# Reordering the query blocks and spreading the projections of an attention and memory kernel

## The chip, the cores and the metric

The kernel runs on one core of a Trainium2 chip. The metric is the device time of one launch in microseconds (us). Engines are called as the profile calls them: PE (matrix multiplication; PEld is its weight load), DVE (vector), ACT (scalar, with the exponentials), POOL (general), SP (here: the queue that issues nearly all DMAs). All data are 32-bit floats.

## The reference

Four sequences (B = 4) of S = 1024 tokens with C = 256 channels pass through four residual steps:

```python
x = x + attn_a(layernorm(x), ...)   # 16 heads of 16 channels, own LayerNorm inside, out-projection with bias
x = x + ffn(layernorm(x), W)        # W rounded to -1, 0, 1 times its mean absolute value
x = x + attn_b(layernorm(x), ...)   # a memory of two 64x64 matrices, updated token by token
x = x + ffn(layernorm(x), W)
```

`attn_a` is full softmax attention: `scores = q k^T / 4`, softmax over the 1024 keys, times v, times `w_out` plus `b_out`, plus its own input. `attn_b` works through the tokens in chunks of 128: keys, values and queries are projections with a causal convolution over four tokens, the gradient of a squared loss of the two matrices at each token is clipped in norm, and two linear recurrences over the tokens (with per-token rates alpha, eta, theta that are themselves means of sigmoids and a softplus of projections) give the matrices that each token's query is answered with. Chunk c needs the state left by chunk c-1 of all four sequences.

## The kernel before, in words

**The main loop.** Queries come in four blocks of 256 (k = 0 to 3), heads in two pairs of groups. A *unit* is (block k, batch b, pair of head groups): 4 x 4 x 2 = 32 units, listed in `units` (L184) with k outermost and b inside it. A unit goes through eight key chunks `kc`, each in two *halves* (`half`, L1207). A half issues, in this order on PE:
- `maxima` (L234): two matmuls of 512 columns (`mx`, L244) for a unit that comes ten key chunks later; DVE reduces them to negated row maxima (`nm`, L248). After a unit's last maxima `maxima_rows` (L250) turns them (`ng`, `nt`), writes them to DRAM (`d`) and reads them back as one row of the queries' tile (`qslot`), so the later scores come out with their maximum subtracted;
- `scores` (L270): eight matmuls of 256 columns (`sc`, L278), whose exponentials ACT takes (`pt`, L284);
- side work (below), after the first half only;
- `weigh` (L288): exponentials times values (`av`, L298), one key chunk late.

The PE, DVE and ACT streams run in the order in which the program issues them; the order of the SP and POOL streams is left to the scheduler of the framework.

**Side work.** Everything else is written as generators that yield between pieces and wait in named *lanes* (`lanes`, L438). `beside(PACE)` (L459) runs pieces of the lanes, in lane order, until a budget of columns is spent: `PACE` = 1200 columns are added per key chunk, and each PSUM tile that a piece takes with `mps` is charged the number given there. If it spent fewer than `LIGHT` = 500, `weigh` is split over the two halves; otherwise it comes whole after the second. `through(lane, ...)` (L477) does the opposite of pacing: it runs all pieces of a lane up to a key at once, between two scores.

**What the side work is.** `project(b)` (L1084) makes a batch's queries, keys and values: load x (two tiles of 4 x 128 tokens), LayerNorm statistics on DVE (L1096, L1097), eight small POOL operations on them (L1102 to L1108, `rr`), the normalised tile `h` on DVE (L1116), 16 transposes on PE (`hps`, L1124), 16 matmuls of 512 columns for queries and keys (`cps`, L1133; ACT adds the bias, SP writes them to DRAM), 16 of 256 for values (`vps`, L1151), and last six long POOL operations that leave x + bias + attention residual in `X` (L1169 to L1172). `other_weights` (L1035) makes the output bias `bo` and the rounded ffn weight; `memory_setup` (L884) loads and transposes the weights of `attn_b` (`wps`, `wpst`, L889; `wops`, `gwps`). `finish` (out-projection `po`, ffn `pf`, both L395), `theta`, `prepare`, `advance`, `retrieve` and `output` do the rest of the layers for a query block once its units are through.

**Where the projections sit.** Batch 0's come before the loop. Those of batches 1, 2 and 3 wait in the lane `before`, and in each unit of the first block this line is met at the fourth key chunk (L1233):

```python
if u + 2 < n0:                                    # n0 = 8, the units of block 0
    through("before", lambda key: key <= units[u + 2][1])
```

So unit 0 runs what is left of batch 1, unit 2 that of batch 2 together with `memory_setup`, and unit 4 that of batch 3, each in one burst between two halves. PE's PSUM is shared as two tiles for maxima (`x`), one for `av` and three for everything else (`m`: scores and side work).

Of the kernel before, what the change touches and what calls it, by code (L numbers as in the profile page):

```python
# [16 lines left out]
P = 128  # L17
# [18 lines left out]
def tile_hybrid(ctx: ExitStack, tc: tile.TileContext, x, ln_gamma, ln_beta, w_qkv, b_qkv, w_out, b_out,  # L36
# [100 lines left out]
    xsp = ctx.enter_context(tc.tile_pool(name="xsp", bufs=1))  # L137
# [41 lines left out]
    def extra(t):  # L179
# [3 lines left out]

    units = [  # L184
        (k, b, tuple(range(g, g + N5 // w)))
        for k, (t0, w) in enumerate(BLOCKS)
        for b in range(B)
        for g in range(0, NG, N5 // w)
# [177 lines left out]
    def finish(b, t, m=2, buf=None):  # L366
# [10 lines left out]
        def turned(src, name):  # L377

            ps = mps([P, 2, m, P], f"{name}p_{n}", 256)
            for e in ts:  # L380
                for cc in range(2):
                    T.transpose(ps[:, cc, e, :], src[:, e, cc * P : (cc + 1) * P], ident)
            if name == "hdT" and t in hids:
                for e in ts:
                    A.copy(hids[t + e][:, :, b, :], ps[:, :, e, :])
                return hids[t][:, :, b : b + 1, :]
            dst = buf("tT", name)[:, :m, :].rearrange("p e c -> p (e c)").rearrange("p (c e t) -> p c e t", c=2, e=m)
            A.copy(dst, ps)  # L388
            return dst

        def times(srcT, w, name):
            ps = mps([P, m, C], f"{name}_{n}", 1024)
# [12 lines left out]

        Xi = X[:, b, t : t + m, :]
# [14 lines left out]
        through("before", lambda key: key <= 2)  # L421
# [4 lines left out]
        tps = mps([P, m, P], f"tps_{n}", 512)  # L426
# [12 lines left out]
        "settle", "finish", "theta", "memory", "ready", "answers", "last", "outputs", "before"  # L439
# [19 lines left out]
    def beside(pace):  # L459

        at["due"] = min(at["due"] + pace, 1500)
        done = 0
        for lane in lanes:
            while lanes[lane] and lanes[lane][0][1] <= at["now"] and at["due"] >= 1 and done < 700:
# [17 lines left out]
    def theta(k, cs):  # L482
# [20 lines left out]
        ps = mps([P, m, 2, 2], f"thp_{k}_{cs.start}", 256)  # L503
# [32 lines left out]
    def prepare(c, g, own):  # L536
# [34 lines left out]
        ps = mps(full, f"natp_{c}", 256)  # L571
# [18 lines left out]
        pa = mps(full, f"pa_{c}", 512)  # L590
# [4 lines left out]
        pe = mps(full, f"pe_{c}", 256)  # L595
# [61 lines left out]
    def advance(c, g, box, own):  # L657
# [86 lines left out]
        if not last:  # L744
# [20 lines left out]
            pw = mps([D, B, D], f"pw_{c}", 160)  # L765
# [42 lines left out]
    def output(c, box, groups, op, add):  # L808
# [23 lines left out]
        for p in pairs:  # L832
            ps = mps([P, 2, C], f"ops_{c}_{p.start}", 512)
# [31 lines left out]
        for p in pairs:  # L865
            ps = mps([P, 2, 2, P], f"oth_{c}_{p.start}", 256)
# [16 lines left out]

    def memory_setup(sp):  # L884

        def transposed(dst, src, rows, name):
            for cc in range(2):
                ps = mps([P, P], f"{name}{cc}")
                T.transpose(ps[:, :rows], src[:rows, cc * P : (cc + 1) * P], ident[:rows, :rows])  # L889
                V.tensor_copy(dst[:, cc, :], ps[:, :rows])  # L890

        with nc.allow_non_contiguous_dma(reason="small constants"):
# [8 lines left out]
            nc.sync.dma_start(b_t[:D, :], tb.rearrange("(p o) -> p o", o=1))  # L901
            nc.sync.dma_start(b_t[D:, :], tb.rearrange("(p o) -> p o", o=1))
# [11 lines left out]
        tn = sp.tile([D, C], F32, tag="nat", name="tn")  # L914
        nc.sync.dma_start(tn, tW)
        transposed(wt, tn, D, "wpst")
        yield 1
# [54 lines left out]
    with tc.manual_schedule(engines=OWN):  # L972
        share(m=8)
        with ExitStack() as s1_:
# [60 lines left out]
            def other_weights(sp):  # L1035

                fw = sp.tile([P, 2, C], F32, name="fw")
                bor = sp.tile([P, C], F32, name="bor")
                nc.sync.dma_start(wo, w_out.rearrange("(cc p) n -> p cc n", p=P))
                nc.sync.dma_start(fw, ffn_w.rearrange("(oc p) i -> p oc i", p=P))  # L1040
# [3 lines left out]
                bvb = sp.tile([P, 2, P], F32, name="bvb")  # L1044
# [6 lines left out]
                yield 1  # L1051
                ones = sp.tile([P, P], F32, name="ones")
# [18 lines left out]
                for ic in range(2):  # L1071
                    ps = mps([P, C], f"fps{ic}")
# [11 lines left out]
            def project(b):  # L1084

                hT = hTp.tile([P, 2, S], F32, tag="hT", name=f"hT_{b}")
# [4 lines left out]
                mv = small.tile([P, NT, 2], F32, tag="mv_a", name=f"mv_a{b}", bufs=1)  # L1091
                r = small.tile([P, 6, NT], F32, tag="rr", name=f"rr_a{b}", bufs=1)
                if b:
                    yield 2
# [14 lines left out]
                yield 3  # L1109
                hs = []  # L1110
                for hf in range(2):
                    h = lnp.tile([P, 4, C], F32, tag="h", name=f"h_{b}_{hf}")
                    hs.append(h)
                    for i in range(4):
# [4 lines left out]
                        if i % 2:  # L1119
                            yield 1 + i // 2  # L1120
                    for cc in range(2):
                        ps = mps([P, N5], f"hps_{b}_{hf}_{cc}", 256)
# [3 lines left out]
                        yield 1  # L1126
                for n in (0, 2, 1, 3):
                    dst = (dq if n < 2 else dk)[b][(n % 2) * P : (n % 2) * P + P, :]
                    for hf in range(2):
                        o = slice(hf * N5, (hf + 1) * N5)  # L1130
                        ps = mps([P, N5], f"cps_{b}_{n}_{hf}", 1024)
                        for cc in range(2):
                            T.matmul(  # L1133
                                ps, lhsT=wg[:, cc, n * P : (n + 1) * P], rhs=hT[:, cc, o], start=cc == 0, stop=cc == 1
                            )
                        c = cmp_.tile([P, N5], F32, tag="c", name=f"c_{b}_{n}_{hf}")
                        A.activation(c, ps, AF.Identity, bias=bqk[:, n : n + 1])  # L1137
                        nc.sync.dma_start(dst[:, o], c)
                        yield 1
                    if b == 0 and n > 1:  # L1140
                        yield "half"
# [4 lines left out]
                for i in range(0, NT, 2):  # L1146
                    ps = mps([P, 2, C], f"vps_{b}_{i}", 1024)
                    for e in range(2):
# [6 lines left out]
                    for e in range(2):  # L1155
# [5 lines left out]
                    yield 1  # L1161
                for g in range(2):
                    nc.sync.dma_start(dv[b][g], v[:, g])
                if b == 0:
                    yield "values"

                for hf, h in enumerate(hs):
                    Xh = X[:, b, 4 * hf : 4 * hf + 4, :]
                    G.tensor_add(Xh, xts[b, hf], bo.unsqueeze(1).to_broadcast([P, 4, C]))  # L1169
                    rh = r[:, 5, 4 * hf : 4 * hf + 4]  # L1170
                    G.tensor_mul(h, h, rh.unsqueeze(2).to_broadcast([P, 4, C]))
                    G.tensor_add(Xh, Xh, h)  # L1172
# [30 lines left out]

            LIGHT, PACE = 500, 1200
# [20 lines left out]
            n0 = sum(1 for k, _, _ in units if k == 0)  # L1225

            def unit(u):
                nonlocal late
                for kc in range(NT):
                    if kc == 0:  # L1230
                        load_keys(u + 1, range(1, 4))
                    if kc == 3:
                        if u + 2 < n0:  # L1233
                            through("before", lambda key: key <= units[u + 2][1])
# [4 lines left out]
                    for pr in range(2):  # L1239
                        half(u, kc, pr)  # L1240
                        if pr == 0:
                            light = beside(PACE) < LIGHT
# [13 lines left out]
            def memory():  # L1256
                for k, (t0, w) in enumerate(BLOCKS[:-1]):
# [4 lines left out]
                    for c in range(c0, c1):  # L1262
# [7 lines left out]
                        if c + 1 < c1:  # L1270
                            load_hid(c + 1)
                            yield 1

            def rest():
# [30 lines left out]
                def ready():  # L1305
                    for c in cs:
# [3 lines left out]
                def chain():  # L1310
                    for c in cs:
# [5 lines left out]

                for c in cs:
# [4 lines left out]
                for c in cs:  # L1323
                    if c + 1 < NT:
                        start("outputs", output(c, box, [slice(0, B)], to_put(c), G.tensor_add))
                    else:
                        of = lambda name, c: ptp.tile([P, B, C], F32, tag="pt", name=f"{name}_{c}")
                        start("last", output(c, box, [slice(0, 2), slice(2, 4)], of, V.tensor_add))

            first = project(0)  # L1330
            for _ in range(5):
                next(first)
            scaled_weights()
            for u in range(2):
                while next(first) != "half":
                    pass
# [3 lines left out]

            def values_first():
                yield from iter(lambda: next(first), "values")
                load_values(0)

# [66 lines left out]
```

## Time and profile before

| | |
|---|---|
| time, median of 3 | 1528.07 us (1520.89 to 1533.3) |
| profiled execution: time, span in the profile | 1524.56 us, 1522.7 us |
| mean granted PE clock | 0.957 |
| PE, DVE, ACT, POOL busy | 94%, 65%, 51%, 17% of the span |
| first scores of unit 0 | 73.7 us |
| units 0 to 9 | 414.8 us |
| units 10 to 29 | 816.3 us |
| unit 30 to the end | 217.9 us |

The page of the profile lists busy times, the span in 40 slices, the DMA queues, the chain of work that ended last, and the costliest groups of instructions as "line engine operation out<-in shapes xcount | busy, mean ns | idle before, what ended it". The trace behind it can be asked for a stretch of time: busy time of each engine, the granted PE clock, the waits, and the single instructions. The rows on unit times above come from the starts of the `mx` and `sc` matmuls in the trace.

### The profile page before, as it was taken

Reading aid. Unit: us, or ns where it says so; the run is one execution under the profiler, and the core shown is the slowest. Engines: PE = TensorE matmul, PEld = TensorE weight load, DVE = VectorE, ACT = ScalarE, POOL = GpSimd, SP = SyncE. Lnnn points to the kernel's source line nnn. Section 1 sums busy time; section 2 is a strip of 40 time slices with the busy share of each in tenths; the row PEclk is TensorE's granted clock in tenths of the full one; section 3 lists DMA queues with packets and bytes.
Section 4 is the critical chain, followed back from the end, with each engine's and each line's share of the span. In section 5 each row is a group of like instructions: output and inputs, shape, how many; then the busy total and the mean of one; then the engine's idle time right before and its main releaser. Section 6 shows DMA issues by size and latency. Waiting matters only on the chain.

```text
span 1522.7 us, 31195 instructions
## 1 busy us (share of the span) xinstructions
PE 1424.4 (94%) x12544; PEld 859.5 (56%) x12544; DVE 987.9 (65%) x1491; ACT 776.4 (51%) x1465; POOL 259.6 (17%) x424
## 2 busy tenths in 40 slices
PE   5979979999999999999999999999999999996886
PEld 3345545565555466565654665666554665664664
DVE  2746628467777785767576867766777767632564
ACT  2034615546565554655566556555566556563242
POOL 6340211200000110112010201210102102111232
PEclk9769979999999999999999999999999999998887
DMA  4512331332122212211213111212222112101000
GB/s 118 154 53 96 98 104 47 101 93 57 54 66 72 65 47 56 64 47 50 71 50 98 57 53 27 59 51 62 56 85 64 55 46 63 39 16 42 21 8 28
DMA packets 82100, 94.91 MB, mean 62 GB/s; under 512 B 32472, under 2 KB 62488, under 8 KB 81956
## 3 DMA queue, kind: packets, MB, share of 16 engines
q1 hardware_dynamic: 81684, 92.14, 20.7%
q8 instruction: 99, 1.62, 0.5%
q10 hardware_dynamic: 272, 0.79, 0.1%
q14 instruction: 45, 0.37, 0.1%
HBM read 60.30 MB, written 30.38 MB: 60 GB/s over the span
## 4 chain that ended last, share of the span: by engine, by line
PE 83%; DVE 7%; ACT 4%; issue 1%; POOL 1%; DMA 1%; SPq 0%; DVEq 0%; POOLq 0%; ACTq 0%
PE mx L244 20%; PE sc L278 19%; PE av L298 16%; PE cps L1133 4%; PE opf L876 2%; DVE nm L248 2%; PE pf L395 2%; PE po L395 2%; PE vps L1151 2%; ACT pt L284 2%; PE gps L820 1%; PE qqps L545 1%; PE tps L428 1%; PE vkps L545 1%; PE hps L1124 1%
## 5 line engine op out<-in xcount | busy, mean ns | idle before, releaser
L284 ACT ACTIVATE pt<-sc 128x512 f32<-128x512 f32 x1024 | 555.3, 594 | 518.0 <-PE sc L278 518.0
L248 DVE TENSOR_REDUCE nm<-mx 128x2 f32<-128x1024 f32 x512 | 619.9, 1221 | 232.4 <-PE sc L278 203.3
L278 PE MATMUL sc<-qslot,kslot 32*128 32x256 f32 x4096 | 647.7, 407 | 4.9 <-ACT m L593 2.5
L244 PE MATMUL mx<-kslot,qslot 32*128 32x512 f32 x2048 | 586.2, 656 | 6.7 <-DVE nm L248 5.7
L278 PEld LDWEIGHTS sc<-qslot,kslot 32*128 32x128 f32 x4096 | 405.5, 187 | 49.8 <-ACT pt L284 9.7
L298 PE MATMUL av<-pt,v 128*32 128x256 f32 x4096 | 302.8, 393 | 4.5 <-DVE a L306 4.4
L244 PEld LDWEIGHTS mx<-kslot,qslot 32*128 32x128 f32 x2048 | 155.9, 187 | 216.5 <-issue 131.0
L298 PEld LDWEIGHTS av<-pt,v 128*32 128x32 f32 x4096 | 96.0, 109 | 150.6 <-issue 114.3
L71 POOL TENSOR_TENSOR rso_hn<-rsi_hn,nhalf 128x2 f32<-128x2 f32 (+1 forms) x17 | 12.0, 707 | 285.0 <-DVE rsi_hn L70 237.4
L1133 PE MATMUL cps<-hT,wg 128*128 128x512 f32 x128 | 56.5, 600 | 0.0
L1160 DVE COPY vtile<-vps 128x256 f32<-128x256 f32 x24 | 9.1, 420 | 58.8 <-PE vps L1151 40.6
L71 POOL TENSOR_TENSOR rso_hd<-rsi_hd,nhalf 128x2 f32<-128x2 f32 (+1 forms) x17 | 12.0, 707 | 193.9 <-DVE rsi_hd L70 124.2
L1133 PEld LDWEIGHTS cps<-hT,wg 128*128 128x128 f32 x128 | 24.5, 194 | 29.3 <-issue 28.5
L876 PE MATMUL opf<-ffn,ohT 128*128 128x256 f32 x128 | 37.2, 440 | 3.0 <-ACT ohT L871 3.0
L1137 ACT ACTIVATE c<-cps,bqk 128x512 f32<-128x512 f32 x32 | 22.0, 687 | 34.3 <-PE cps L1133 30.2
L877 DVE TENSOR_TENSOR gt<-X,opf 128x512 f32<-128x512 f32 x16 | 11.0, 687 | 43.1 <-PE opf L876 43.1
L395 PE MATMUL pf<-ffn,hnT 128*128 128x256 f32 x124 | 32.0, 401 | 2.3 <-ACT hnT L388 2.3
L876 PEld LDWEIGHTS opf<-ffn,ohT 128*128 128x128 f32 x128 | 26.3, 216 | 12.1 <-ACT ohT L871 4.2
L395 PE MATMUL po<-wo,aT 128*128 128x256 f32 x128 | 32.3, 394 | 0.0
L820 PE MATMUL gps<-gwT,hid 128*128 128x256 f32 x128 | 31.2, 389 | 0.2 <-ACT pt L284 0.2
L1151 PE MATMUL vps<-wg,hT 128*128 128x256 f32 x128 | 29.2, 382 | 0.0
L395 PEld LDWEIGHTS pf<-ffn,hnT 128*128 128x128 f32 x124 | 22.7, 194 | 10.1 <-issue 5.0
(354 smaller groups left out, 1460.0 us busy)
## 6 DMA issues: line engine op xcount, KB each, us to landing
v<-dv SPq DMA_DIRECT2D x32, 604.0 KB
kslot<-dk SPq DMA_DIRECT2D x256, 64.0 KB
da<-a SPq DMA_DIRECT2D x31, 256.0 KB
dv<-vtile SPq DMA_DIRECT2D x8, 604.0 KB
x<-in_L_attn_a_x_dram SPq DMA_DIRECT2D x8, 512.0 KB
dq<-c SPq DMA_DIRECT2D x16, 256.0 KB
qslot<-dq SPq DMA_DIRECT2D x256, 16.0 KB
dk<-c SPq DMA_DIRECT2D x16, 256.0 KB
```

Source lines behind the costliest of these rows:

```text
L71: G.tensor_tensor(out=r[:, :n], in0=t[:, :n], in1=nhalf[:, :n], op=ALU.pow)
L244: T.matmul(ps[:, e, :], lhsT=qS[u][o : o + SL, j * P : (j + 1) * P], rhs=kt[o : o + SL, hf * N5 : (hf + 1) * N5], start=True, stop=True,)
L248: V.tensor_reduce(nms[u][:, hf, 2 * pr : 2 * pr + 2, j], ps, AX.X, ALU.max, negate=True)
L278: T.matmul(ps[e][:, g * w : (g + 1) * w], lhsT=kS[u, g][o : o + SL, kc * P : (kc + 1) * P], rhs=qS[u][o : o + SL, g * w : (g + 1) * w], st ...
L284: A.activation(pt[:, e, :], ps[e], AF.Exp, scale=1.0 / HD**0.5)
L298: T.matmul(avs[u][SL * i : SL * (i + 1), part * w : (part + 1) * w], lhsT=v[:, kc, o : o + SL], rhs=pts[u, kc, i // 2][:, i % 2, part * w ...
L395: T.matmul(ps[:, e, :], lhsT=srcT[:, cc, e, :], rhs=w[:, cc, :], start=cc == 0, stop=cc == 1)
L545: T.matmul(ps, lhsT=w[:, cc, :], rhs=hidT[:, cc], start=cc == 0, stop=cc == 1)
L820: T.matmul(ps[:, e, :], lhsT=hidT[:, cc, p.start + e, :], rhs=gwT[:, cc, :], start=cc == 0, stop=cc == 1)
L876: T.matmul(pf[:, e, :], lhsT=hT[:, cc, e, :], rhs=ffn[:, cc, :], start=cc == 0, stop=cc == 1)
L1133: T.matmul(ps, lhsT=wg[:, cc, n * P : (n + 1) * P], rhs=hT[:, cc, o], start=cc == 0, stop=cc == 1)
L1151: T.matmul(ps[:, e, :], lhsT=hT[:, cc, o : o + P], rhs=wg[:, cc, 2 * C :], start=cc == 0, stop=cc == 1,)
```

## The change

- **Order of units.** Block 1 of batch 0 is put directly behind block 0 of batch 0; the others keep their order. `n0` becomes 10 and the last unit of block 0 is unit 9.
- **Projections.** `project` is split: `input_stats(b)` (loads, statistics, the eight POOL operations) is a generator in a lane of its own, `stats`, started one batch ahead; `project` waits for it. For batches 1 to 3 the queries and keys come in pieces of 256 columns instead of 512 (32 matmuls a batch instead of 16), the values one tile of 128 tokens a piece. `through` at the fourth key chunk is replaced by `needed(b, stage)`, which runs pieces of a batch only up to the stage that the coming units need: queries and keys of the first pair of groups, of both, and values.
- **Residual sums.** The six long POOL operations move from the end of `project` to right behind each half of `h`; batch 0's stay behind the output bias.
- **Weights.** `other_weights` is split into `output_bias` (before the loop) and `last_weights`; `theta_setup` is cut out of `memory_setup`; these three go into a new lane `weights`, last in line, and are no longer run in a burst.
- **Pacing.** 900, 1000 and 1250 columns per key chunk for units 0 to 11, 12 to 23 and the rest; unspent budget up to 3000 columns instead of 1500; up to 800 columns a time instead of 700 (more while over 2000 are due); the charges of many tiles are set anew. The lane order changes.

The diff, cut to its core:

```diff
     units = [
-        (k, b, tuple(range(g, g + N5 // w)))
-        for k, (t0, w) in enumerate(BLOCKS)
-        for b in range(B)
-        for g in range(0, NG, N5 // w)
+        (k, b, tuple(range(g, g + N5 // BLOCKS[k][1])))
+        for k, b in sorted(((k, b) for k in range(len(BLOCKS)) for b in range(B)), key=lambda o: (o[0] if o != (1, 0) else 0, o[1]))
+        for g in range(0, NG, N5 // BLOCKS[k][1])
     ]
...
     lanes = {name: [] for name in (
-        "settle", "finish", "theta", "memory", "ready", "answers", "last", "outputs", "before"
+        "settle", "finish", "theta", "outputs", "memory", "ready", "answers", "last", "stats", "before", "weights"
     )}
...
-        at["due"] = min(at["due"] + pace, 1500)
+        at["due"] = min(at["due"] + pace, 3000)
...
-            while lanes[lane] and lanes[lane][0][1] <= at["now"] and at["due"] >= 1 and done < 700:
+            while lanes[lane] and lanes[lane][0][1] <= at["now"] and at["due"] >= 1 and (done < 800 or at["due"] > 2000):
...
-            def project(b):
-
-                hT = hTp.tile([P, 2, S], F32, tag="hT", name=f"hT_{b}")
+            def input_stats(b):
+
                 for hf in range(2):
                     if (b, hf) not in xts:
                         load_x(b, hf)
...
                 if b:
-                    yield 2
+                    yield 6 if b == 1 else 3
                 for i in range(NT):
                     V.bn_stats(st[:, i, :], xts[b, i // 4][:, i % 4, :])
                     V.bn_aggr(mv[:, i, :], st[:, i, :])
...
+                normed_by[b] = mv, r
+
+            def residual_sums(b, hf, h):
+
+                mv, r = normed_by[b]
+                Xh = X[:, b, 4 * hf : 4 * hf + 4, :]
+                rh = r[:, 5, 4 * hf : 4 * hf + 4]
+                G.tensor_mul(Xh, h, rh.unsqueeze(2).to_broadcast([P, 4, C]))
+                G.tensor_add(Xh, Xh, bo.unsqueeze(1).to_broadcast([P, 4, C]))
+                G.tensor_add(Xh, Xh, xts[b, hf])
+
+            def project(b):
+
+                hT = hTp.tile([P, 2, S], F32, tag="hT", name=f"hT_{b}")
+                while b not in normed_by:
+                    yield 0.5
+                mv, r = normed_by[b]
                 hs = []
...
+                    if b:
+                        residual_sums(b, hf, h)
...
+                if b and b + 1 < B:
+                    start("stats", input_stats(b + 1))
                 for n in (0, 2, 1, 3):
                     dst = (dq if n < 2 else dk)[b][(n % 2) * P : (n % 2) * P + P, :]
-                    for hf in range(2):
-                        o = slice(hf * N5, (hf + 1) * N5)
-                        ps = mps([P, N5], f"cps_{b}_{n}_{hf}", 1024)
+                    w = N5 if b == 0 else N5 // 2
+                    for o in range(0, S, w):
+                        ps = mps([P, w], f"cps_{b}_{n}_{o}", 2 * w)
...
+                    if n > 1:
+                        reached[b] = n - 1
...
-                for hf, h in enumerate(hs):
-                    Xh = X[:, b, 4 * hf : 4 * hf + 4, :]
-                    G.tensor_add(Xh, xts[b, hf], bo.unsqueeze(1).to_broadcast([P, 4, C]))
-                    rh = r[:, 5, 4 * hf : 4 * hf + 4]
-                    G.tensor_mul(h, h, rh.unsqueeze(2).to_broadcast([P, 4, C]))
-                    G.tensor_add(Xh, Xh, h)
+            def needed(b, stage):
+
+                while reached.get(b, 0) < stage:
+                    piece("stats" if lanes["stats"] and b not in normed_by else "before")
...
-            LIGHT, PACE = 500, 1200
+            LIGHT = 500
+            PACES = (900, 1000, 1250)
...
-                        if u + 2 < n0:
-                            through("before", lambda key: key <= units[u + 2][1])
+                        for v, stage in ((u + 2, 1), (u + 1, 3)):
+                            if v < U:
+                                needed(units[v][1], min(stage + units[v][2][0] // 2, 3))
...
-                            light = beside(PACE) < LIGHT
+                            light = beside(pace(u)) < LIGHT
...
-                start("before", values_first(), -1)
-                start("before", sums_first(sp2), 0)
+                start("before", first, 0)
                 for b in range(1, B):
                     start("before", project(b), b)
-                    if b == 2:
-                        start("before", memory_setup(sp2), b)
                 for _ in range(NT + LEAD):
                     for pr in range(2):
                         half(None, None, pr)
                         beside(1000)
-                through("before", lambda key: key < 0)
+                needed(0, 3)
+                load_values(0)
+                start("weights", last_weights(*setting), 0)
+                start("weights", theta_setup(*setting), 0)
+                start("weights", memory_setup(*setting), 1)
```

## Prediction

> **What bounds the kernel now.** I read the page first, then the stretches of the main loop, then who PE waits for, then the inside of the three bursts. Five lines of the page:
>
> ```profile
> PE 1424.4 (94%) x12544; PEld 859.5 (56%) x12544; DVE 987.9 (65%) x1491; ACT 776.4 (51%) x1465; POOL 259.6 (17%) x424
> ...
> PE   5979979999999999999999999999999999996886
> ...
> PEclk9769979999999999999999999999999999998887
> ...
> PE 83%; DVE 7%; ACT 4%; issue 1%; POOL 1%; DMA 1%; SPq 0%; DVEq 0%; POOLq 0%; ACTq 0%
> ```
>
> PE carries the chain and is full nearly everywhere, so time can only be won where PE is idle, where its clock is low, or where its matmuls stall. Past the start (slices 1, 2) and before the end, slices 3 and 6 (38 us each) are such places, by their PE or PEclk digit: they hold the bursts of units 0 and 2. PE's waits in the stretch 73 to 500 us (us, times, longest) name the causes:
>
> ```profile
> PE hps L1124 <- DVE h L1116: 10.3, 1, 10.3
> PE wps L889 <- DMA nat<-in_L_attn_b_eW_dram: 3.3, 1, 3.3
> PE wps L889 <- DMA nat<-in_L_attn_b_Wq_dram: 3.1, 1, 3.1
> ...
> PE wpst L889 <- DMA tn<-in_L_attn_b_tW_dram: 2.2, 1, 2.2
> ```
>
> Now the windows (stretch, length, busy us of PE, PEld, DVE, ACT, POOL, granted clock, DMA):
>
> ```profile
> 158.64:162.23 3.59, 3.59 (x45) 2.02 (x41) 3.17 (x6) 2.17 (x5) 0.00 (x0) 1.00 0.02 2
> 324.54:329.65 5.11, 5.11 (x53) 3.33 (x49) 3.55 (x8) 2.29 (x5) 0.00 (x0) 1.00 0.17 39
> 86.31:126.11 39.80, 29.51 (x127) 18.06 (x123) 12.62 (x35) 10.71 (x18) 17.38 (x13) 0.83 0.28 90
> 90.50:100.70 10.20, 0.00 (x0) 0.00 (x0) 5.09 (x20) 0.46 (x1) 4.37 (x7) 0.60 0.00 0
> 100.70:106.80 6.10, 6.03 (x20) 4.42 (x21) 2.19 (x7) 2.35 (x4) 3.61 (x2) 0.54 0.55 172
> 183.41:219.37 35.96, 27.43 (x113) 16.19 (x109) 8.84 (x28) 8.07 (x13) 6.55 (x3) 0.90 0.41 132
> 219.37:229.71 10.34, 10.34 (x61) 4.62 (x60) 5.24 (x19) 2.67 (x5) 0.00 (x0) 0.53 0.05 13
> 286.80:310.30 23.50, 23.50 (x97) 13.98 (x93) 4.69 (x10) 8.29 (x14) 4.24 (x2) 1.00 0.38 113
> ```
>
> In order: a plain pair of halves; a pair that also holds one `po`; burst 1 with its pair; its idle gap and the cold clock behind it; burst 2; the cold clock behind it; burst 3. The last has PE full at clock 1.00: a burst as such loses nothing, its waits do.
>
> **The change part by part** (against the profiled 1524.56 us; span 1522.7).
>
> *Burst 1, unit 0.* Its pair would take 3.59, `hps` 2.3 (16 transposes, 0.58 for four in the paced halves), `cps` and `vps` 20.8 (the trace: 13.74 and 7.0 in burst 2). 39.8 - 26.7 = **13.1 lost**: 10.3 idle while DVE does eight bn_stats/bn_aggr pairs (90.88 to 95.2), POOL the eight `rr` operations (95.56 to 100.3, two powers of 1.67 each) and DVE the first `h` (100.21); the other 2.8 is the clock. In the changed program the statistics come from the lane `stats`, two tiles between two maxima, a unit before the `hps`: the chain of 10 us lies beside about ten halves of PE. Uncovered it would cost the 10.3 again.
>
> *Burst 2, unit 2.* The projections end at 206.4; from there to 219.37 `memory_setup` takes 13.0 for about 2.5 of transposes at full clock. The three halves after it take 4.72, 3.03, 2.59 where 1.65, 1.94, 1.88 is usual: 4.9. Together **15.4 lost**. In the changed order each pair of `wps` stands one key chunk (over 3.6 us) behind the one that frees its `nat` tile; the waits were 3.1 and 3.3 long. I take all of it as gained; if SP is late with these loads, up to 5 comes back.
>
> [...] The window 90.50 to 100.70 has no matmul, and the clock stays near one half to 106.8: 6 us. Behind burst 2 it is 0.53 over 10.34 us. [...] The rows give 2.8 + 4.9 = 7.7. [...]
>
> *Burst 3* has nothing to win in waits.
>
> *Pacing instead of bursts.* A plain pair is 3.59 though its matmuls need less: the second half stands about 0.29 until `pt` frees a scores tile. A pair with a `po` (4 matmuls of 256 columns) takes 5.08 to 5.11: 1.5 more, while the same columns in a burst took 13.74/8 = 1.72. So a key chunk that takes projection work wins about 0.23. The changed order of PE has such pieces in about 31 key chunks of units 1 to 7: **-7**. The splitting of `cps` into 256 columns is in the price of `po`, which has that shape. Five of eight `vps` pieces still run together at the fourth key chunk of units 3, 5 and 7, at burst price.
>
> *Start.* Batch 1's `x` loads now stand in SP's queue, with four `qslot` loads, ahead of the `d` of unit 0's maxima. The second x load waits for POOL's residual sums to free its tile: four of 2.35 us behind `bo` (about 59.9) end at 69.2; with the loads behind it `d` goes out at about 72 instead of 69.2. The first scores (73.7 before) wait for it: **+2.9**. `fps` leaves the cold halves of unit 0: **-1**.
>
> *Residual sums beside the loop.* Six POOL operations per batch (1.89 + 2.35 + 2.35 per half) now run while DVE does maxima. Two queues stand behind them. SP's next x load waits for them, but is wanted by bn_stats some 10 us later (a wait there would hold the `nm` behind it on DVE, and with it PE). And DVE itself:
>
> ```profile
> L1066 DVE TENSOR_SCALAR pos<-fw,sc 128x512 f32<-128x512 f32 x1 | 2.5, 2480 | 0.0
> ...
> L1068 DVE TENSOR_SCALAR fw<-fw,sc 128x512 f32<-128x512 f32 x1 | 0.5, 528 | 0.0
> ```
>
> These two have one shape; the first ran beside a POOL residual sum and took 1.95 longer. The reduction `nm` kept its 1.22 at such times. [...] The second half's `h` is a tensor_scalar and follows the first half's sums by about a key chunk. [...] The page's row has DVE idle 232.4 us over 512 `nm`, 0.45 each, so a hit of 1.95 would cost PE about 1.5, and two or three of six half batches should be hit: **+4**, ends 0 and 14 (nine hits).
>
> *Steady part, units 10 to 29.* Same work with other paces. Besides the plain price of halves I find some 36 us of stalls there (halves of 4 to 6 us where `theta`'s logarithm and the chunk work meet on ACT). The changed order has three such meetings too. **0**, ends -10 and +10.
>
> *End.* The last units carry nearly the same PE sequence; unit 31 gets about 2.8 us more of chunk work, part of it covered because unit 31 has no maxima left: **+2**, ends 0 and 4. The block order shifts work between units 2 to 9 without adding any; memory's first chunk starts two units later but is paced well ahead of the end: 0.
>
> Sum: -13.1 - 15.4 - 7 + 2.9 - 1 + 4 + 0 + 2 = **-27.6**, so 1497.0 on the profiled execution. The median of before is 3.5 above its profiled run; on that basis **1500 us**.
>
> **Rivals.**
> - *A, forecast, 0.62:* 1490 to 1511.
> [...]
> [...]
> - *D, slower, 0.05:* the x loads come late. If POOL's sums (6.6 per half) and the load behind them take longer than the 10 us of lead, DVE stands in bn_stats, `nm` stands behind it, and PE after two halves. It decides from about 11 us of standing at each of the four halves of x of batches 2 and 3 on (43 over the forecast); at 12 it gives 1548. Against: the sums and the load together would have to come 20 us after their issue, with the DMA engines 21% busy over the span.
> - That the change doesn't do what it says is shut out by the order of the PE stream: the pieces do stand between scores.
>
> **How the numbers follow.** A measurement of this kernel can tell about 1% (15 us) from no change: faster ends at 1512.8, slower begins at 1543.4. A and C lie below the first but for a small part, B is split across it, D lies above the second. That gives 0.83, 0.12, 0.05. The range, with the bounds of lock, steady part and end added up as independent: 1481 to 1517.
>
> **What would show it.** No wait of `hps` on `h` over 1 us; no `wps` on DMA; clock 1.00 from unit 1 on. First scores near 76.6; units 0 to 9 about 382 instead of 414.8, 10 to 29 about 816, unit 30 to the end about 220. [...] The forecast is wrong if units 0 to 9 stay over 400, or units 10 to 29 move by over 10.

## The result, and the profile after

The changed kernel takes 1531.14 us (median of 20 runs, 1525.12 to 1536.3) against 1524.8 us (20 runs, 1518.72 to 1533.3). The ratio is **1.0033, interval 1.0017 to 1.0048**: a third of a per cent slower, where 1.8% faster was forecast. The profiled execution spans 1530.2 us, 7.5 more than before.

The lines of its page that answer to those shown of before:

```profile
PE 1431.0 (94%) x12640; PEld 871.4 (57%) x12640; DVE 994.4 (65%) x1491; ACT 781.7 (51%) x1489; POOL 257.2 (17%) x424
...
PE   5999898999999999999999999999999999996886
...
PEclk9889999999999999999999999999999999998887
...
PE 80%; DVE 8%; ACT 6%; DMA 1%; issue 1%; POOL 1%; SPq 0%; DVEq 0%; POOLq 0%; ACTq 0%
```

The dips of slices 3 and 6 are gone, but the fifth and seventh slices have an 8 now, and the chain has lost 3% of PE to DVE and ACT. PE's waits from 73 to 500 us, as they were asked for before:

```profile
PE cps L1168 <- ACT c L1172: 4.6, 2, 4.1
PE sc L279 <- DMA qslot<-d: 2.4, 1, 2.4
PE gwps L936 <- DVE woT L933: 2.3, 2, 1.3
PE wps L889 <- DMA nat<-in_L_attn_b_eW_dram: 1.6, 1, 1.6
```

The wait of 10.3 on `h` is gone, as forecast, and of the three on weight loads one is left, at 1.6 instead of 3.3; the other three lines are new. The stages of the span (start; units 0 to 9; 10 to 29; the end), in the columns of the windows shown before:

```profile
0.00:80.51 80.51, 58.16 (x192) 28.45 (x193) 39.13 (x57) 11.72 (x21) 32.06 (x68) 0.89 0.39 118
80.51:481.84 401.33, 387.55 (x3649) 237.14 (x3649) 263.76 (x392) 211.93 (x406) 62.90 (x69) 0.98 0.26 79
481.84:1309.08 827.24, 805.40 (x7635) 482.69 (x7631) 587.88 (x827) 470.08 (x891) 111.20 (x204) 0.99 0.21 57
1309.08:1530.20 221.12, 179.94 (x1178) 123.12 (x1174) 103.66 (x217) 88.00 (x173) 51.08 (x84) 0.88 0.09 27
```

Against before (73.8, 414.7, 816.5, 217.7): +6.7 at the start, -13.4 in units 0 to 9, **+10.7 in units 10 to 29**, +3.4 at the end. The forecast had +2.9, -32.5, 0 and +2. Both signs that it named for being wrong came: units 0 to 9 stay over 400, and units 10 to 29 move by over 10.

Three places account for much of the first two. **The start.** Instructions of SP, POOL and PE, "start, us, engine, line, operation" and what released them:

```profile
63.99 4.64 POOL L1132 TENSOR_TENSOR X<-X,bo 128x1024 f32<-128x1024 f32 x2 [28.24 <-DVE bo L1057]
68.58 4.64 POOL L1133 TENSOR_TENSOR X<-X,x 128x1024 f32<-128x1024 f32 x2
70.95 2.70 SPq L997 DMA_DIRECT2D x<-in_L_attn_a_x_dram  x2
73.70 1.88 SPq L223 DMA_DIRECT2D qslot<-dq  x4
75.69 0.37 SPq L262 DMA_DIRECT2D d<-nt  x1
80.51 2.50 PE L279 MATMUL sc<-qslot,kslot 32*128 32x256 f32 x8 [2.43 <-DMA qslot<-d]
```

The residual sums now read x last, so the two x loads wait for the third and the fourth of these POOL operations, and `d`, whose data was ready at 71.2 (`nt` at 70.99 took 0.21), stands behind them on SP. **Unit 2, fourth key chunk**, on SP, ACT and PE:

```profile
159.10 0.37 SPq L321 DMA_DIRECT2D da<-a  x1
163.92 0.58 SPq L323 DMA_DIRECT2D dn<-da  x1
164.55 1.06 SPq L325 DMA_DIRECT2D aT<-da  x2
165.71 0.40 SPq L1173 DMA_DIRECT2D dq<-c  x1
166.20 3.90 SPq L1173 DMA_DIRECT2D dk<-c  x4
169.28 0.47 ACT L1172 ACTIVATE c<-cps,bqk 128x256 f32<-128x256 f32 x1 [5.41 <-DMA dq<-c]
169.80 1.65 PE L1168 MATMUL cps<-hT,wg 128*128 128x256 f32 x3 [4.07 <-ACT c L1172]
```

A unit's result goes to DRAM (`da`) and is read back (`dn`, `aT`). SP stands in that round trip from 159.5 to 163.9; behind it are the stores of `c`. There are four `c` tiles, as before the change, but each now holds only 256 columns; ACT finds none free, and PE waits for ACT. The clock falls then too, as the windows of the pair's first half and of its second show (granted clock 0.69 and 0.77):

```profile
164.59:173.52 8.93, 4.86 (x22) 3.22 (x21) 2.34 (x6) 1.92 (x4) 0.00 (x0) 0.69 0.33 104
173.52:176.16 2.64, 2.64 (x29) 1.55 (x28) 0.89 (x1) 1.28 (x3) 0.00 (x0) 0.77 0.52 152
```

**Unit 3**: its four pairs of halves from 217.12 to 243.24, which hold the pieces of `memory_setup`, take 26.12. By the prices of the same pieces in other units (17.2 without the setup, as in `e3_setup` below) and the forecast's 2.5 for the setup they would take about 19.5, by estimate.

### The profile page after: what moved, and what is told of

Read it like the earlier page. It is cut to its first block, busy times and chain, and to the rows that moved or that the text cites. A ratio compares the mean times of both kernels' runs of the same rounds, so it can differ in the third digit from the quotient of the medians.

```text
span 1530.2 us, 31461 instructions
## 1 busy us (share of the span) xinstructions
PE 1431.0 (94%) x12640; PEld 871.4 (57%) x12640; DVE 994.4 (65%) x1491; ACT 781.7 (51%) x1489; POOL 257.2 (17%) x424
## 4 chain that ended last, share of the span: by engine, by line
PE 80%; DVE 8%; ACT 6%; DMA 1%; issue 1%; POOL 1%; SPq 0%; DVEq 0%; POOLq 0%; ACTq 0%
PE mx L245 19%; PE sc L279 19%; PE av L299 16%; PE cps L1168 3%; DVE nm L249 2%; PE opf L878 2%; PE po L396 2%; PE vps L1189 2%; ACT pt L285 2%; PE pf L396 2%; PE gps L822 1%; PE tps L430 1%; PE qqps L547 1%; DVE qq L564 1%; DVE vk L564 1%
## 5 line engine op out<-in xcount | busy, mean ns | idle before, releaser
L279 PE MATMUL sc<-qslot,kslot 32*128 32x256 f32 x4096 | 640.3, 405 | 8.8 <-DMA qslot<-d 2.4
L279 PEld LDWEIGHTS sc<-qslot,kslot 32*128 32x128 f32 x4096 | 396.7, 186 | 62.5 <-ACT pt L285 9.7
L299 PE MATMUL av<-pt,v 128*32 128x256 f32 x4096 | 295.4, 391 | 2.9 <-DVE a L307 2.9
L299 PEld LDWEIGHTS av<-pt,v 128*32 128x32 f32 x4096 | 99.8, 109 | 145.1 <-issue 106.6
L1168 PE MATMUL cps<-hT,wg 128*128 128x256 f32 (+1 forms) x224 | 65.7, 438 | 4.9 <-ACT c L1172 4.6
L1168 PEld LDWEIGHTS cps<-hT,wg 128*128 128x128 f32 x224 | 40.8, 196 | 26.5 <-issue 13.2
L1172 ACT ACTIVATE c<-cps,bqk 128x256 f32<-128x256 f32 (+1 forms) x56 | 27.9, 505 | 28.1 <-PE cps L1168 14.9
L564 DVE SCALAR_TENSOR_TENSOR qq<-rqq,cw_qq,qq 128x512 f32<-128x512 f32 x21 | 20.0, 952 | 19.2 <-ACT qq L562 18.8
L396 PE MATMUL po<-wo,aT 128*128 128x256 f32 x128 | 32.5, 396 | 0.0
L307 DVE COPY a<-av 128x512 f32<-128x512 f32 x32 | 21.8, 681 | 13.4 <-PE av L299 13.4
L1189 PEld LDWEIGHTS vps<-wg,hT 128*128 128x128 f32 x128 | 23.2, 189 | 9.1 <-issue 4.5
```

What stands on the lines that cost most here:

```text
L279: T.matmul(ps[e][:, g * w : (g + 1) * w], lhsT=kS[u, g][o : o + SL, kc * P : (kc + 1) * P], rhs=qS[u][o : o + SL, g * w : (g + 1) * w], st ...
L299: T.matmul(avs[u][SL * i : SL * (i + 1), part * w : (part + 1) * w], lhsT=v[:, kc, o : o + SL], rhs=pts[u, kc, i // 2][:, i % 2, part * w ...
L396: T.matmul(ps[:, e, :], lhsT=srcT[:, cc, e, :], rhs=w[:, cc, :], start=cc == 0, stop=cc == 1)
L564: V.scalar_tensor_tensor(out=y, in0=r[:, :, j : j + P], scalar=cw[:, j : j + 1], in1=y, op0=ALU.mult, op1=ALU.add)
L1168: T.matmul(ps, lhsT=wg[:, cc, n * P : (n + 1) * P], rhs=hT[:, cc, o : o + w], start=cc == 0, stop=cc == 1)
L1189: T.matmul(ps[:, e, :], lhsT=hT[:, cc, o : o + P], rhs=wg[:, cc, 2 * C :], start=cc == 0, stop=cc == 1,)
```

## The experiments

The first runs weigh a theory, "new waits": the old stalls were worth about what the forecast gave, and waits that the forecast had at nothing or too small took their place. Against it stand two others: that the removed stalls were never worth their length, and that stalls only move. Units 10 to 29 have a question of their own: is it the pacing or the order of blocks that slows them?

Stages of every run's profiled execution in us, from the starts of the scores. Each is one execution; the ratios rest on 4 to 20 executions of the kernel, and where the table says "one execution" there is no ratio:

| kernel | first scores | units 0-9 | units 10-29 | unit 30 to end | span | ratio (interval) |
|---|---|---|---|---|---|---|
| before | 73.8 | 414.7 | 816.5 | 217.7 | 1522.7 | |
| changed | 80.5 | 401.3 | 827.2 | 221.1 | 1530.2 | 1.0033 (1.0017-1.0048) |
| b12_waits | 74.1 | 395.3 | 809.9 | 219.2 | 1498.5 | 0.9876 (0.9839-0.9914) |
| b3_paces | 75.7 | 415.7 | 824.7 | 209.5 | 1525.6 | 1.0044 (1.0029-1.0059) |
| e6_oldpaces | 80.3 | 401.5 | 814.7 | 223.2 | 1519.7 | 1.0005 (0.9987-1.0024) |
| c1_threewaits | 71.7 | 392.0 | 824.0 | 221.8 | 1509.5 | 0.9903 (0.9871-0.9935) |
| e1_sums | 74.1 | 401.8 | 823.0 | 222.0 | 1520.9 | one execution |
| e2_stores | 80.5 | 394.4 | 826.9 | 222.1 | 1524.0 | one execution |
| e3_setup | 80.0 | 406.8 | 824.7 | 222.0 | 1533.5 | one execution |
| c2_all | 74.6 | 391.9 | 817.4 | 216.4 | 1500.2 | 0.9900 (0.9878-0.9921) |
| e4_lane | 81.1 | 406.4 | 833.2 | 222.4 | 1543.1 | 1.0093 (1.0062-1.0123) |
| e5_budget | 80.8 | 402.1 | 825.5 | 228.8 | 1537.2 | 1.0060 (1.0023-1.0096) |
| d1_oldorder | 76.2 | 420.1 | 817.2 | 224.3 | 1537.8 | 1.0080 (1.0046-1.0113) |
| c3_nat2 | 74.8 | 389.1 | 817.1 | 223.2 | 1504.2 | 0.9870 (0.9836-0.9904) |
| c1_again | 74.3 | 391.2 | 824.0 | 221.1 | 1510.5 | 0.9940 (0.9917-0.9963) |
| c2_again | 75.1 | 395.2 | 818.8 | 219.4 | 1508.5 | 0.9882 (0.9853-0.9910) |

**b12_waits: the kernel before without the two waits.** Its edit:

```diff
+                yield from first          # other_weights: batch 0's sums right behind bo
...
+                    if u == 0 and kc < 3:
+                        for _ in range((3, 2, 1)[kc]):
+                            next(ahead)   # ahead = project(1)
...
-            t = sp.tile([P, C], F32, tag="nat", name=f"nat{n}")
+            t = sp.tile([P, C], F32, tag=f"nat{n}", name=f"nat{n}")
...
-        tn = sp.tile([D, C], F32, tag="nat", name="tn")
+        tn = sp.tile([D, C], F32, tag="tn", name="tn")
```

> The kernel before, with its three bursts, block order and pacing kept, and only the two waits inside the bursts taken away: batch 1's statistics are issued in the three key chunks of unit 0 ahead of its burst, and each weight tile of memory_setup has a buffer of its own, so that its load can go early. Theory 'new waits' (the removed stalls were worth what the forecast gave them, and the changed kernel lost as much elsewhere): units 0 to 9 fall from 414.8 to about 390, units 10 to 29 stay at 816, the whole falls by about 23 us, ratio 0.985. Rival 'the stalls were never worth their length' (what PE does not wait for there, it waits for in the next units): units 0 to 9 fall by under 8, ratio 0.995 or more.

Units 0 to 9 fell by 19.4, unit 0 by 10.0 and unit 2 by 9.4; the ratio is 0.9876. The stalls were worth most of their length, and with the bursts left in place the kernel gained as much as the best of the spread kernels below (0.9870). Two things stayed. In burst 1 the first `h` still comes late:

```profile
PE hps L1125 <- DVE h L1117: 2.3, 1, 2.3
```

The other is seen behind burst 2, in the windows of its pair and of the next:

```profile
171.75:201.28 29.53, 28.59 (x135) 17.12 (x131) 10.02 (x29) 9.40 (x16) 6.55 (x3) 1.00 0.43 146
201.28:208.70 7.42, 7.42 (x44) 3.19 (x43) 4.10 (x18) 1.64 (x3) 0.00 (x0) 0.54 0.12 44
```

PE is idle for 0.9 in the first, and still the next pair has a granted clock of 0.54 and takes 7.42 instead of 3.59.

**b3_paces and e6_oldpaces: the pacing put into the one kernel, taken out of the other.** The core of the first edit (the second is its reverse, in the changed kernel):

```diff
-        "settle", "finish", "theta", "memory", "ready", "answers", "last", "outputs", "before"
+        "settle", "finish", "theta", "outputs", "memory", "ready", "answers", "last", "before"
...
-        at["due"] = min(at["due"] + pace, 1500)
+        at["due"] = min(at["due"] + pace, 3000)
...
-                            light = beside(PACE) < LIGHT
+                            light = beside(900 if u < 12 else 1000 if u < 24 else 1250) < LIGHT
```

> The kernel before with only the change's pacing: 900, 1000 and 1250 columns, up to 3000 due, 800 at a time, the new charges, and 'outputs' ahead of 'memory' among the lanes. Theory 'pacing' (the slower units 10 to 29 of the changed kernel come from how chunk work is dealt out, which brings ACT and DVE work of two lanes together): units 10 to 29 go from 816 to about 827, units 0 to 9 stay, ratio about 1.007. Rival 'block order' (they come from memory starting two units later, so that its work stands denser): under 3 us, ratio 1.000 to 1.002.

> The changed kernel with the old pacing (1200 columns, 1500 due, 700 at a time, old charges except those of the new projection pieces) and the old lane order. Theory 'pacing': units 10 to 29 come back from 827 to about 816, the whole falls by about 10 us from the changed kernel's 1531. Rival 'block order': they stay within 3 us of 827.

Units 10 to 29 rose by 8.2 in the first and fell by 12.5 in the second; the ratios moved by +0.44% and -0.28% (4 to 7 us; the intervals of the second pair overlap by a little). So the slow stretch comes with the pacing and not with the block order. The old kernel gave part back at the end (209.5: its chunk work was further ahead), the changed one did not.

**c1_threewaits, and its parts e1_sums, e2_stores, e3_setup.**

```diff
+                if b == 0:                       # e1: the old order, x is free after two sums
+                    G.tensor_add(Xh, xts[b, hf], bo.unsqueeze(1).to_broadcast([P, 4, C]))
+                    G.tensor_mul(h, h, rh.unsqueeze(2).to_broadcast([P, 4, C]))
+                    G.tensor_add(Xh, Xh, h)
+                    return
...
-                        c = cmp_.tile([P, w], F32, tag="c", name=f"c_{b}_{n}_{o}")
-                        A.activation(c, ps, AF.Identity, bias=bqk[:, n : n + 1])
-                        nc.sync.dma_start(dst[:, o : o + w], c)
+                        oc = o % N5              # e2: two pieces in one tile and one store
+                        if oc == 0:
+                            c = cmp_.tile([P, N5], F32, tag="c", name=f"c_{b}_{n}_{o}")
+                        A.activation(c[:, oc : oc + w], ps, AF.Identity, bias=bqk[:, n : n + 1])
+                        if oc + w == N5:
+                            nc.sync.dma_start(dst[:, o - oc : o + w], c)
...
+        while at["unit"] < 7:                    # e3: memory_setup waits for unit 7
+            yield 1
```

> The changed kernel with three new waits taken away: (1) batch 0's residual sums in the old order of operations, which frees the x tiles two POOL operations earlier, so x loads and with them the d of unit 0 go out some 4 us earlier; (2) two 256-column pieces of cps share one tile and one store to DRAM, so ACT does not run out of c tiles while SP waits for a unit's da; (3) memory_setup begins in unit 7. Theory 'new waits': -4 at the start (first scores near 77 instead of 80.5), -6 in unit 2, -5 in unit 3, about -15 from the changed kernel, ratio to the kernel before about 0.994. Rival 'the stalls only move': first scores as said, but units 0 to 9 within 4 us of 401.

> The changed kernel with one thing undone: batch 0's residual sums in the old order of operations (x + bo first), so that the x tiles are free after the first two sums instead of after all. Theory 'SP queue at the start': x loads go out at about 66 and 69 us instead of 71 and 73, d of unit 0 at about 71.5 instead of 75.7, first scores at 76 or earlier instead of 80.5; the rest of the loop as it was (U0 to U9 about 401). Rival 'cold clock' (the start is late because PE runs its maxima at half clock): first scores within 1 us of 80.5.

> The changed kernel with two 256-column pieces of cps in one tile and one store. Theory 'c tiles run out while SP stands at dn<-da': the wait of ACT's c (5.4 us) and of cps behind it (4.1 us) at the fourth key chunk of unit 2 goes, unit 2 takes about 43 instead of 49.1. Rival 'ACT is simply full there': unit 2 stays within 1.5 us of 49.1.

> The changed kernel with memory_setup held back until unit 7. Theory 'setup pieces wait on loads, DVE and PSUM': unit 3 falls from 51.6 to about 44 and unit 1 by 1; units 7 to 8, where the pieces now stand, rise by 4 to 5 (their matmuls are 2.5, with one or two load waits of 1.6 to 3). [...]

Together they took the changed kernel from 1.0033 to 0.9903. The parts:

*e1.* First scores at 74.1 instead of 80.5. The same instructions as above:

```profile
61.66 4.64 POOL L1132 TENSOR_TENSOR X<-x,bo 128x1024 f32<-128x1024 f32 x2 [27.87 <-DVE bo L1057]
64.02 2.69 SPq L997 DMA_DIRECT2D x<-in_L_attn_a_x_dram  x2
66.25 4.64 POOL L1134 TENSOR_TENSOR X<-X,h 128x1024 f32<-128x1024 f32 x2
70.60 0.34 SPq L262 DMA_DIRECT2D d<-nt  x1
```

The x loads go 6.9 earlier, of which 2.3 are `bo`, that came earlier itself in this execution; `d` goes 5.1 earlier. The queue at the start is shown.

*e2.* Unit 2 took 42.9 instead of 49.1 (-6.2), and `cps` no longer waited for `c` there. The whole path of the stall, SP to ACT to PE, hung on how many tiles and stores the pieces use.

*e3* missed. Unit 3 fell by 11, unit 4 rose by 11.5 and units 5 to 9 by 10.9: with the setup out of the way the pieces were dealt out anew, seven pieces of `cps` came in one key chunk of unit 4, and ACT stood 5.0 for a free `c` tile there, the stores behind eight `qslot` loads on SP. Only together with e2's edit does the rise go (unit 4: 45.1 in c1), and what is left of the gain is small: c1's units 0 to 9 are 2.4 below what e2 alone gave.

**c2_all: both together.** Its edit is that of c1 and of e6.

> The changed kernel without the three new waits and with the old pacing and lane order. If the two losses are separate they add up: units 0 to 9 about 392, units 10 to 29 about 814, ratio to the kernel before about 0.986. If the stalls only move: no better than 0.990, the ratio without the three waits alone.

Units 10 to 29 came down to 817.4, but the ratio did not show it (0.9900 on five executions).

**e4_lane and e5_budget: the pacing in halves.**

> The changed kernel with only the old lane order ('outputs' behind the memory's lanes and 'answers'). [...]

> The changed kernel with only the old budget: 1200 columns, 1500 due, 700 at a time and the old charges; the new lane order stays. Theory 'column budget': units 10 to 29 fall from 827 to about 818. Rival 'lane order': they stay above 824.

Neither half brings the gain back: with half of the pacing undone the changed kernel is slower still, 1.0093 and 1.0060, and units 10 to 29 take 833.2 and 825.5. Neither the lane order nor the budget is the cause by itself. That it is how the pieces of different lanes fall together, dealt out anew by each half put back alone, is argued, not shown.

**d1_oldorder: c2 with the old order of units.**

```diff
-        for k, b in sorted(((k, b) for k in range(len(BLOCKS)) for b in range(B)), key=lambda o: (o[0] if o != (1, 0) else 0, o[1]))
+        for k, b in ((k, b) for k in range(len(BLOCKS)) for b in range(B))
```

> The kernel without the three new waits and with old pacing (the last run of the second set), and with the old order of units too: block 1 of batch 0 comes after block 0 of batch 3. If moving that block is what makes room (batch 1 is wanted two units later, so that its projections can be paced), its queries and keys must now run in a burst in unit 0 again, with DVE, POOL and DMA in front of it: units 0 to 9 about 10 to 12 us more than 392, ratio about 0.997. If pacing and early statistics alone carry the gain: within 4 us of 392.

Units 0 to 9 take 420.1 instead of 391.9, over twice the expected loss, and unit 0 alone 66.8: PE waits there 10.1 for `h`, as before the change. So in the spread kernel the moved block is what gives batch 1's statistics the time to be early. `b12_waits` got them early without it, and what moving the block does alone was not run.

**c3_nat2: c2 with two buffers for the weight tiles.**

```diff
-            t = sp.tile([P, C], F32, tag="nat", name=f"nat{n}")
+            t = sp.tile([P, C], F32, tag=f"nat{n % 2}", name=f"nat{n}")
```

> As the kernel without the three new waits and with old pacing, but with two buffers for the weight tiles of memory_setup, so that each load can go while the one before is transposed. The wait of wps on the load in unit 7 (its pairs stand 2 to 3 us over their price) goes: unit 7 about 3 us shorter, ratio 0.988. If these pairs are slow for DVE's copies and PSUM instead: no change from 0.990.

The wait of `wps` on its load is gone, units 5 to 9 take 193.9 instead of 196.3. At 0.9870 it is, with b12_waits, the fastest kernel here (c2_again's 0.9882 is not told apart from them). The longest PE waits left from 73 to 500 us:

```profile
PE gwps L938 <- ACT pt L285: 1.2, 2, 0.6
PE gwps L938 <- DVE woT L935: 1.0, 2, 0.7
PE wps L889 <- ACT pt L285: 0.9, 3, 0.6
```

**c1_again and c2_again.** The pair that could not be told apart, repeated on one chip in five rounds.

> The changed kernel without the three new waits, new pacing kept, a second time and beside the next run on one chip. If pacing costs 4 to 7 us by itself: ratio to the kernel before about 0.991. If it costs nothing once the waits are gone: the same as the next run within 0.002.

> The same with the old pacing and lane order. If pacing costs 4 to 7 us: 0.987, that is 0.003 to 0.005 under the run before it. If it costs nothing: within 0.002 of it.

0.9940 with the new pacing, 0.9882 with the old: 0.58% apart, about 9 us, and the intervals do not meet. The pacing costs time by itself; the first pair, c1 and c2_all on four and five executions, had not shown it (0.9903 and 0.9900).

## Why the prediction was wrong, point by point

Of the 35 us between -27.6 and +7.5: +3.8 at the start, +19.1 in units 0 to 9, +10.7 in units 10 to 29, +1.4 at the end. The steps that failed are the stores of `c`, which had no term at all (6.2); `memory_setup` between the halves (about 6.6 over its price); the count of key chunks that pacing would make cheaper (about 5 of the 7 did not come); and the steady part, put at 0. The first three are 17.8 of the 19.1 in units 0 to 9; but the residual sums' +4 did not come either, so some 5 there stay unexplained.

- **"Start: +2.9."** Right in mechanism, mis-sized: +6.7. The text had POOL's four sums end at 69.2; `bo` was ready at 63.8, 3.9 later than taken, and they ended at 73.2. That the x loads behind these sums hold the first scores, e1 shows; why `bo` was late stays open.
- **"Uncovered waits of bursts 1 and 2: -28.5."** They vanished as said: no wait of `hps` on `h` over 1 us. Taking the same waits away in the old kernel gave 19.4, and b12_waits shows what is missing. For burst 1 it was 10.0 of 13.1, with the wait of 2.3 left in. For burst 2 it was 9.4 of 15.4: the slow clock behind it stays (a pair takes 7.42 at a granted clock of 0.54, where a plain pair takes 3.59 at 1.00), so the term "the three halves after it: 4.9", which took the waits for the cause of the slow clock, was wrong in its cause; and the setup's matmuls, with waits of 0.7 left, still take 4.2 (197.1 to 201.3) where 2.5 was taken. So the waits themselves were worth about their length.
- **"Pacing instead of bursts: -7."** The price holds, the count doesn't. A paced pair with two pieces of `cps` in unit 2 takes 5.10, just as the pair with `po`; the last pair of unit 2, with two pieces too, takes 5.89; and a pair of unit 3 with seven pieces of `vps` takes 9.63:

```profile
148.21:153.31 5.10, 5.10 (x53) 3.16 (x49) 2.45 (x3) 3.06 (x7) 0.00 (x0) 1.00 0.74 208
191.43:197.32 5.89, 5.89 (x54) 3.73 (x50) 3.69 (x5) 4.48 (x10) 4.16 (x8) 1.00 0.27 73
207.50:217.13 9.63, 9.63 (x74) 6.88 (x70) 6.11 (x10) 3.45 (x7) 1.13 (x3) 1.00 0.05 15
```

  The last is about a plain pair (3.59) and seven eighths of the 7.0 that eight pieces take in a burst. Of the 72 pieces of `cps` and `vps` in the changed kernel 34 stand in pairs with three to eight of them, ahead of the fourth key chunk of units 2 to 7, where `needed` runs what is due, and these take burst price. The forecast counted about 31 cheaper key chunks, with runs of five `vps` only; ten pairs with two pieces took 5.08 to 5.24. At 0.21 each that is about 2, not 7. The kernel without the new waits (c3_nat2) agrees: PE waits little there, and its units 0 to 9 take 389.1 where the forecast has 382.
- **The step that failed first: the queues.** The prediction followed SP for the x loads and for `d`, but not for the stores of `c`, though these are part of every moved piece. A burst issues all its stores in a row; spread over units, they stand behind each unit's round trip `da` to `dn`. That was worth 6.2 (e2).
- **"`memory_setup`: I take all of it as gained; if SP is late, up to 5 comes back."** It came back, and more: 26.12 for pairs of 19.5. One load wait of 1.6 was in it; the rest is `gwps` and `wps` behind DVE's copies and ACT, which wait in line with `h`, `aT` and `pt`. Moved to unit 7, which takes 39.2 without it, the setup costs 9.4 in c1 (48.6) and with a second buffer 5.5 in c3 (44.7), still over the 2.5.
- **"Residual sums beside the loop: +4."** `h` did meet the sums on POOL, at about the cost to DVE that the row gave (1.95), but not to PE. In unit 5, with `h` beside a sum:

```profile
323.99 2.97 DVE L1147 TENSOR_SCALAR h<-x,mv_a,rr_a 128x256 f32<-128x256 f32 x2
324.46 2.35 POOL L1133 TENSOR_TENSOR X<-X,x 128x1024 f32<-128x1024 f32 x1
```

  the second of the two `h` took 2.51 instead of 0.40. In units 0 to 9 I find five such operations, 5.4 us over their medians; PE's waits on `nm` from 73 to 500 us are 0.4 in all, so the +4 for PE did not come. The range counts with a "lock": no run shows one, and what the runs showed are these longer times, the largest 2.51 instead of 0.40.
- **"Steady part: 0, ends -10 and +10."** Another step that failed. +10.7 in the profile, and 4 to 9 us by the ratios of three pairs of kernels (b3 and before, changed and e6, c1_again and c2_again). It was put at nothing because the counts of work are the same; but a budget and a lane order decide what meets. One such meeting, in unit 15, windows and instructions:

```profile
683.52:689.42 5.90, 3.07 (x24) 2.13 (x20) 5.83 (x6) 1.53 (x3) 4.41 (x3) 1.00 0.10 26
```

```profile
683.39 4.52 DVE L564 SCALAR_TENSOR_TENSOR qq<-rqq,cw_qq,qq 128x512 f32<-128x512 f32 x3
683.55 2.79 POOL L856 TENSOR_TENSOR X<-X,gt 128x1024 f32<-128x1024 f32 x1 [7.56 <-DVE gt L852]
689.42 0.70 PE L245 MATMUL mx<-kslot,qslot 32*128 32x512 f32 x2 [2.83 <-DVE nm L249]
```

  `output`'s sum on POOL fell on `prepare`'s convolution on DVE (4.52 for three of 0.75), and PE stood 2.83 for a maximum. A slowing of DVE beside POOL, which the prediction priced for the residual sums, did its harm here, between two pieces that the change did not touch. This one pair is 4 of the 10.7, and it is not the whole of the cause: with the old lane order (e4_lane) the meeting is gone, and units 10 to 29 take 833.2 all the same. The `qq` of the changed kernel and of e4_lane (count, then busy us and mean ns):

```profile
L564 DVE SCALAR_TENSOR_TENSOR qq<-rqq,cw_qq,qq 128x512 f32<-128x512 f32 x18 | 17.7, 985 | 14.7 <-ACT qq L562 14.2
L564 DVE SCALAR_TENSOR_TENSOR qq<-rqq,cw_qq,qq 128x512 f32<-128x512 f32 x18 | 13.5, 752 | 10.5 <-ACT qq L562 10.1
```

  The clock has a part too. In units 10 to 29 the clock records of the traces stand at half (0.5) for 24 us in the changed kernel, 17 before and 3 in e6_oldpaces; the means there are 0.99, 0.99 and 1.00. If a us at half clock costs half a us, an estimate from the granted share, that is 3.4 of the 10.7, but 10.2 of the 12.5 by which e6 is faster here. What makes up the rest stays open.
- **"End: +2."** It was +3.4, inside the bounds of 0 to 4.

New waits in the engines' order did come, and those that counted were at the stores of `c` (6.2) and in `memory_setup` (about 6.6).

## What to carry to other kernels

Before spreading a burst, look for the waits in it: taking them away (statistics earlier, buffers of their own) gave 1.2% here with four small edits, and the spreading gave no more. Work that is moved into a steady loop brings its stores along, so follow them through the queue to whatever in that loop makes the queue stand, and count the buffers that have to last so long. Changing a pacing rule over the whole kernel has a price of its own, found only by running it alone: a schedule that is tuned piece by piece is dealt out anew.

## What the runs showed of the hardware

In these traces the granted clock is not foretold by PE's idle time alone. It fell in unit 2 of the changed kernel during a gap of 4.1 us (from 1.00 to 0.50, at 167.9 us, for 6.8 us), but in b12_waits right behind a burst in which PE was idle for 0.9 us of 29.5, with about four us of transposes at its end (1.00 in the burst, 0.54 in the 7.42 us behind it). And units 10 to 29, with the same pieces in the same key chunks, ran 816.5 us at a mean clock of 0.99 in the kernel before and 809.9 us at 1.00 in b12_waits. The first has three stretches of half clock there, 17 us together, and the second none. The four executions of b12_waits run from 1500.29 to 1509.29 us. A difference of under ten us in one profiled execution of this kernel is thus not yet a finding, and the verdicts above on pacing rest on the ratios.

```profile
469.40:1279.30 809.90, 792.33 (x7664) 479.61 (x7661) 588.29 (x822) 466.23 (x884) 117.92 (x210) 1.00 0.21 59
```
